# Attention scores in one full-height matmul instead of passes over 32 rows, with heads made four at a time and a loop ordered by a clock model

## The chip, the cores and the metric

The kernel runs on one core of a Trainium2 chip. The metric is the device time of one execution in microseconds, as the median of several runs.

## The reference

Two transformer-like layers work on x of shape (2, 1024, 256), that is 2048 rows of 256 values. Layer 0 is linear attention (16 heads of 16) and a gated feed-forward block with ternary weights, layer 1 is softmax attention with rotary position and a gated feed-forward block whose weights pass a Hadamard transform; each sublayer normalises its input and adds its output to x in the kernel. What this change touches is the attention of layer 1:

```
q = (x @ q_w.T + q_b) in 16 heads of 16; k and v the same; q, k rotated by position
attn  = einsum('bhqd,bhkd->bhqk', q, k) * 16 ** -0.5        # 1024 x 1024 per head
probs = softmax(attn, axis=-1)
out   = einsum('bhqk,bhkd->bhqd', probs, v); then out @ out_w.T + out_b
```

With 2 batches and 16 heads there are 32 such score matrices.

## The kernel before

**Units.** Attention of layer 1 goes by eight units: a batch and a group of four heads (`units`). A unit has 1024 queries, in two halves n of 512, and 1024 keys, in eight blocks of 128. Three kinds of work make one unit.

1. *Search.* For each block of 128 queries, half of the keys and two heads, a score tile `scm` [128 queries, 2, 512 keys] goes to PSUM, and VectorE takes its maximum over the keys (`scores_max`, tile `peak`). There are 32 such pairs of heads in a unit. After 16 pairs `split_peaks` makes the negated maxima into a high and a low fp32r part (`tops`), and `put_peaks` transposes them (tile `mx`).
2. *Weights.* For each block of 128 keys, 512 queries and two heads, the transposed score tile `sce` [128 keys, 2, 512 queries] goes to PSUM with the negated maximum already added, and ScalarE makes `pr` = exp(sce / 4). Again 32 pairs in a unit.
3. *Sums.* `weigh` multiplies `pr` of four heads by the values `va` (16 columns and a one, 17 in all) into four 32-column strips of one PSUM bank, `po`, in fp32. After eight key blocks `po` is transposed back, divided by the sum of weights (`normalise`, `divide`), and after four units of a batch projected by `wo1` (`project`, tile `py<-woT,aT`).

**Exactness.** TensorE handles fp32r in one pass and fp32 in four. q and k are kept as fp32r high and low parts. A head has 32 rows: in `kk` the 16 high and 16 low rows of k; in `qh` the high part of q twice; in `ql` the low part twice. A score tile is then two passes of 32 rows (`qh`, `ql`), and a weight tile three, the third being `ones_r` against `mx`. Four heads lie in the four 32-row strips of the array. `burst` issues the passes of a search pair (two strips) and of a weight pair (the other two) in turns, so that four matmuls run beside each other: ten matmuls in three steps.

**Heads.** `heads_of(b, gg)` makes eight heads (two units) at once, for one block of 128 rows at a time: a projection of 384 columns (`pqkv`), bias on VectorE, rotation on GpSimd and VectorE, splitting, four transposes (`pt`, of `rot` in fp32 and of `ks` in fp32r), then one ScalarE copy to `qk_hi` and one VectorE subtraction to `ql`.

**Order.** Two mechanisms. The front (layer 0 for all but two pieces of its feed-forward, normalisation, the first heads, the whole search of unit 0) is recorded in a `Plan`: `Plan.emit` schedules all recorded operations by their estimated cost, with a table `LEADS` of leads per group and engine. After that comes the loop over units, written out by hand: each step issues a burst for unit u+1's search and unit u's weights, then `slot` fills TensorE with other work in proportion to what is left: `filler` (the rest of layer 0, the Hadamard transforms `pw`, layer 1's feed-forward, tiles `pug` and `py<-wd,hid`), `urgent` (the next heads), `background`, and work due after some steps (`later`). Generators yield marks (SOON, FIRST, SECOND, LAST, PAIR, BOTH) that say at which places of a step they may go on. Two sums are issued after every fourth pair.

**PSUM.** Of eight banks `po` has one, three rotate as `bank`, and two tiles of two banks rotate as `pair`, which scm and sce take in turns.

Every recorded operation is issued in the helper `emit`, so that the profile gives all of them the line L316; the tiles' names tell them apart.

Of the kernel before, what the change touches and what calls it, by code (L numbers as in the profile page):

```python
# [82 lines left out]
BURST = 0.65  # L83
# [15 lines left out]
class Root:  # L99


    def __init__(self, make, n, dtype, ring, before, grain):
        self.make, self.dtype, self.ring, self.before, self.grain = make, dtype, ring, before, grain
        self.tile = None
        self.sums = False
        self.placed = False
        self.ready = np.zeros(n)
        self.writer = np.full(n, -1)
        self.readers, self.adders, self.users = [], [], []
# [48 lines left out]
class Plan:  # L158
    def __init__(self):
        self.ops = []  # L160
        self.open = None
        self.burst = False
        self.group("norm 0a")
        self.holds, self.later = [], set()
# [16 lines left out]
    def add(self, engine, call, name, args, kw):  # L181
        if engine == PE and self.open is not None:
            op = self.open
        else:
            op = Op(len(self.ops), engine, self.leads[ENGINES.index(engine)])
            self.ops.append(op)
            self.open = op if engine == PE else None
            if self.burst:
                op.cost = BURST
# [8 lines left out]
        if not self.burst:  # L198
            op.cost += cost(engine, name, outs[0], ins)
# [72 lines left out]
class Pool:  # L272
# [5 lines left out]
    def tile(self, shape, dtype, tag, name, bufs=None):  # L278
# [9 lines left out]
        )  # L288
        if self.state.plan is None:
            root.get()  # L290
# [3 lines left out]
class Engine:  # L294
# [5 lines left out]
    def __getattr__(self, name):  # L300
        call = getattr(self.engine, name)

        def go(*args, **kw):
            if self.state.plan is None or self.which is None:
                return emit(call, args, kw)
# [5 lines left out]
class State:  # L311
    plan = None

# [5 lines left out]
class Ring:  # L319


    def __init__(self, n, in_order):
        self.places, self.next, self.latest, self.in_order = [None] * n, 0, None, in_order

# [16 lines left out]
def cost(engine, name, out, ins):  # L341
    n = out.ids.size
    if engine == PE:
# [3 lines left out]
        return ins[1].ids.size * (PASS if single else COL)  # L347
# [9 lines left out]

@with_exitstack
def tile_two_layers(ctx: ExitStack, tc: tile.TileContext, a: dict, out: bass.AP):
# [5 lines left out]
    ordered = [False]  # L365
# [10 lines left out]
    ps = open_pool(ctx, "ps", 1, 2 * C, space=PSUM)  # L376
    ident = const.tile([P, P], F32, tag="ident", name="ident")
# [3 lines left out]
    def pair(name):  # L381
        return ps.tile([P, 2, C], F32, tag="pair", name=name, bufs=2)


    taken, in_use, now = [0], {}, [None]

    def has_room():
        return len(in_use) < 3

    def bank(name):  # L390
        while ordered[0] and not has_room():
            go(in_use[min(in_use)])
        t = ps.tile([P, C], F32, tag="bank", name=name, bufs=3)
        if ordered[0]:
            in_use[taken[0]] = now[0]
            t.root.number = taken[0]
            taken[0] += 1
        return t

    def shut(t):  # L400

        if ordered[0]:
            del in_use[t.root.number]

    po = ps.tile([P, C], F32, tag="po", name="po", bufs=1)
    vector.memset(po, 0.0)
# [55 lines left out]
    SOON, FIRST, SECOND, LAST, PAIR, BOTH = 1, 2, 3, 4, 5, 6  # L462

# [26 lines left out]
    def norm_T(src, dst, pause=0.0):  # L490
# [5 lines left out]
        for j in range(CT):  # L496
            vector.bn_stats(stats[:, j, :], src[:, j, :])
            vector.bn_aggr(mv[:, j, :], stats[:, j, :])
            if j == 1:
                yield 0.0, SECOND  # L500
        vector.tensor_scalar_add(rstd, mv[:, :, 1], LN_EPS)
        gpsimd.tensor_tensor(rstd, rstd, minus_half, ALU.pow)
        yield 0.0, SECOND
        vector.scalar_tensor_tensor(shift, mv[:, :, 0], -1.0, rstd, ALU.mult, ALU.mult)
        xn = at.tile([P, CT, D], F32, tag="stage", name="xn", bufs=3)
        for j in range(CT):
# [3 lines left out]
            if j == 1:  # L510
                yield 0.0, SECOND
        yield pause, SECOND
        yield 0.0
        for k in range(2):
            pt = bank("pt")
            for j in range(CT):
                tensor.transpose(pt[:, j * P : (j + 1) * P], xn[:, j, k * P : (k + 1) * P], ident)
            yield CT * P * TR, SOON
            (vector.tensor_copy if k else scalar.copy)(dst[:, k, :], pt)
            shut(pt)  # L520
            yield 0.0


    def ffn(cc, first, second, half_scale, scale, down, before_down):
# [4 lines left out]
        for e in range(NB):  # L529
            cols = slice(e * P, (e + 1) * P)  # L530
            pug = bank("pug").rearrange("p (w n) -> p w n", w=2)
# [13 lines left out]
            yield F * COL, SOON  # L545
# [7 lines left out]
            yield 0.0  # L553
        before_down()
        for j in range(F // P):
            t = at // P + j
            cols = slice(j * P, (j + 1) * P)
            py = bank("py")[:, 0:D]
# [4 lines left out]
            yield D * COL, SOON  # L563
            vector.tensor_add(xc[c][:, t, :], py, xc[c][:, t, :])
            shut(py)
            yield 0.0

    def run(gen):
        for _ in gen:
            pass  # L570

    def cost_of(x):
        return x[0] if isinstance(x, tuple) else x
# [20 lines left out]
    both = at.tile([P, 4, E], F32, tag="qk_hi", name="both", bufs=1)  # L594
    for n, k, m, t, r in (
        ("wuT0", D, E, "wA", both[:, 0:2, :]),
        ("wgT0", D, E, "wB", both[:, 2:4, :]),
        ("wdT0", E, D, "wC", at.tile([P, NB, D], F32, tag="ql", name="wdT0", bufs=1)),
# [11 lines left out]
    trig = load(const, "trig", a["trig"], [P, BT, 2, HD // 2])  # L610
# [139 lines left out]
    def ffn0(cc, before_down, wide=False, by_pool=False):  # L750
# [21 lines left out]
        for e in range(0, NB, step):  # L772
# [4 lines left out]
            else:  # L777
                pug = bank("pug").rearrange("p (w b n) -> p w b n", b=1, w=2)
# [15 lines left out]
            yield 4 * F * PASS, SOON  # L794
# [8 lines left out]
            yield 0.0  # L803
        before_down()

# [12 lines left out]
        yield 2 * D * PASS, SOON  # L818
# [4 lines left out]
        yield 0.0  # L823
# [9 lines left out]
    def norm1(c, pause=0.0):  # L833
        yield from norm_T(xc[c], xnT[c], pause)

        for j in range(0, CT, 2):
            x2 = xc[c][:, j : j + 2, :]
            gpsimd.tensor_tensor(x2, x2, ob1.unsqueeze(1).to_broadcast([P, 2, D]), ALU.add)

# [6 lines left out]
    qh, ql, kk, va, mx = {}, {}, {}, {}, {}  # L846
    late = []

    head_tiles = {}

    def heads_of(b, gg, first=0, last=BT):

        if (b, gg) not in head_tiles:
            pool = late[0] if gg else at
            thk = pool.tile([P, 4, S], F32R, tag="qk_hi", name="qk_hi", bufs=1)
            tl = pool.tile([P, 2, S], F32R, tag="ql", name="ql", bufs=1)
            tv = pool.tile([P, BT, HH, VW], F32, tag="va", name="va", bufs=1)

            gpsimd.memset(tv[:, :, :, HD:], 1.0)
            for i in range(2):  # L860
                g = 2 * gg + i
                qh[b, g], ql[b, g], kk[b, g] = thk[:, i, :], tl[:, i, :], thk[:, 2 + i, :]
                va[b, g] = tv[:, :, 4 * i : 4 * i + 4, :]
            head_tiles[b, gg] = thk, tl, tv
        thk, tl, tv = head_tiles[b, gg]
        half = HD // 2
        w3 = slice(gg * 3 * P, (gg + 1) * 3 * P)
        bias = qkvb[:, w3]

        def lay_out(i, rot, ks):  # L870
            cols = slice(i * P, (i + 1) * P)
            pt = bank("pt").rearrange("p (g n) -> p g n", g=4)
            for g in range(2):
                q4 = rot[:, 4 * g : 4 * g + 4, :, :].rearrange("p h s d -> p (h s d)")
                tensor.transpose(pt[:, g, :], q4, ident)
                k4 = ks[:, 4 * g : 4 * g + 4, :, :].rearrange("p h s d -> p (h s d)")
                tensor.transpose(pt[:, 2 + g, :].bitcast(F32R), k4, ident_r)
            return cols, pt

        def take_out(cols, pt):  # L880
            scalar.copy(thk[:, :, cols], pt)
            vector.tensor_tensor(tl[:, :, cols], pt[:, 0:2, :], thk[:, 0:2, cols], ALU.subtract)
            shut(pt)

        def split_k(i):
            rot, a0, b1 = made[i]
            del made[i][1:]
            vector.tensor_tensor(rot[:, :, :, 0:half], a0, b1, ALU.subtract)
            ks = at.tile([P, HH, 2, HD], F32R, tag="ks", name="ks")
            scalar.copy(ks[:, :, 0, :], rot[:, HH:, 0, :])  # L890
            gpsimd.tensor_tensor(ks[:, :, 1, :], rot[:, HH:, 1, :], ks[:, :, 0, :], ALU.subtract)
            made[i].append(ks)


        made = {}
        for i in range(first, last + 2):
            if i >= first + 2:
                cols, pt = lay_out(i - 2, *made.pop(i - 2))
                yield 3 * P * TR
                take_out(cols, pt)  # L900
            if i >= last:
                yield 0.0, LAST
                if i == last:
                    split_k(i - 1)
                    yield 0.0, PAIR
                continue
            c, j = divmod(b * BT + i, CT)
            qk = at.tile([P, 2 * HH, 2, half], F32, tag="qk", name="qk", bufs=1)
            if state.plan:
                plan.with_place(qk)  # L910
            pqkv = bank("pqkv")[:, 0 : 3 * P]
            for k in range(2):
                tensor.matmul(
                    pqkv,
                    lhsT=xnT[c][:, k, j * P : (j + 1) * P],
                    rhs=wqkv[:, k, w3],
                    start=(k == 0),
                    stop=(k == 1),
                )
                if k == 0:  # L920
                    yield 3 * P * COL
            yield 3 * P * COL, LAST
            if i > first:
                split_k(i - 1)
            yield 0.0, FIRST
            vector.tensor_add(qk.rearrange("p h t f -> p (h t f)"), pqkv[:, 0 : 2 * P], bias[:, 0 : 2 * P])
            vector.tensor_add(
                tv[:, i, :, 0:HD],
                pqkv[:, 2 * P :].rearrange("p (h d) -> p h d", d=HD),
                bias[:, 2 * P :].rearrange("p (h d) -> p h d", d=HD),  # L930
# [3 lines left out]
                trig[:, i, s, :].unsqueeze(1).unsqueeze(1).to_broadcast([P, 2 * HH, 2, half]) for s in range(2)  # L934
# [616 lines left out]
```

## Time and profile before

| what | value |
|---|---|
| median of 3 runs | 870.12 us (868.38 to 872.65) |
| profiled execution | 873.07 us, span 871.3 us |
| mean granted TensorE clock | 0.989 |
| first weight burst (tile sce) | 206.1 us from the span's start |
| last sums of po end | 862.8 us, 8.5 us before the end |

The profile is of one execution. PE is TensorE's matmul row, PEld its weight loads, DVE VectorE, ACT ScalarE, POOL GpSimd, SP SyncE, which issues all DMAs here. A group line ends with busy time and mean duration of one, then the engine's idle time just before these instructions and what ended it. A matmul line of the timeline names the tile that is written and the tiles that are read, and the rows and columns of the array that it uses (32*128 is 32 rows). An fp32 matmul shows as two instructions of two passes. Durations of matmuls overlap, since they are pipelined.

### The profile page before, as it was taken

Reading aid. Unit: us, or ns where it says so; the run is one execution under the profiler, and the core shown is the slowest. Engines: PE = TensorE matmul, PEld = TensorE weight load, DVE = VectorE, ACT = ScalarE, POOL = GpSimd, SP = SyncE. Lnnn points to the kernel's source line nnn. Section 1 sums busy time; section 2 is a strip of 40 time slices with the busy share of each in tenths; the row PEclk is TensorE's granted clock in tenths of the full one; section 3 lists DMA queues with packets and bytes.
Section 4 is the critical chain, followed back from the end, with each engine's and each line's share of the span. In section 5 each row is a group of like instructions: output and inputs, shape, how many; then the busy total and the mean of one; then the engine's idle time right before and its main releaser. Section 6 shows DMA issues by size and latency. Waiting matters only on the chain.

```text
span 871.3 us, 14418 instructions
## 1 busy us (share of the span) xinstructions
PE 840.0 (96%) x5952; PEld 499.5 (57%) x5952; DVE 587.6 (67%) x979; ACT 440.5 (51%) x649; POOL 220.7 (25%) x293
## 2 busy tenths in 40 slices
PE   7999999999999999899999999999999999999997
PEld 5689866576556534555455555555555555555543
DVE  5887665886895687557775767687665666666312
ACT  6745455523664556445553445445454544444663
POOL 2646867621551551103510000045000000000000
PEclk9999999999999999999999999999999999999998
DMA  9200000000000200000000000000100000000001
GB/s 312 91 1 2 2 1 1 1 25 1 1 26 2 97 1 1 1 1 2 1 1 2 1 1 1 1 2 7 43 1 2 1 1 1 2 1 1 1 2 48
DMA packets 10768, 14.88 MB, mean 17 GB/s; under 512 B 1104, under 2 KB 8912, under 8 KB 10704
## 3 DMA queue, kind: packets, MB, share of 16 engines
q1 hardware_dynamic: 10704, 13.98, 4.7%
q8 instruction: 46, 0.75, 0.3%
q14 instruction: 18, 0.15, 0.1%
HBM read 11.88 MB, written 2.10 MB: 16 GB/s over the span
## 4 chain that ended last, share of the span: by engine, by line
PE 81%; DVE 13%; ACT 2%; issue 2%; DMA 1%; POOL 1%; SPq 0%; DVEq 0%; ACTq 0%; POOLq 0%
PE pug L316 17%; PE scm L316 15%; PE py L316 14%; PE po L316 13%; PE sce L316 8%; DVE peak L316 5%; PE pqkv L316 5%; PE pt L316 3%; PE pkv L316 2%; DVE act L316 1%; PE sc L316 1%; PE pq L316 1%; DVE att L316 1%; ACT pr L316 1%; PE pw L316 1%
## 5 line engine op out<-in xcount | busy, mean ns | idle before, releaser
L316 ACT ACTIVATE pr<-sce 128x1024 f32<-128x1024 f32 x256 | 260.6, 1024 | 266.0 <-PE sce L316 265.6
L316 DVE TENSOR_REDUCE peak<-scm 128x2 f32<-128x1024 f32 x224 | 273.9, 1223 | 152.0 <-PE scm L316 149.3
L316 PE MATMUL po<-pr,va 128*17 128x512 f32 x1024 | 124.8, 595 | 0.1
L316 PE MATMUL sce<-qk_hi 32*128 32x512 f32 x512 | 121.7, 497 | 1.1 <-ACT pr L316 0.9
L316 PE MATMUL scm<-qk_hi 32*128 32x512 f32 x448 | 112.5, 498 | 6.5 <-DVE peak L316 5.7
L316 PEld LDWEIGHTS scm<-qk_hi 32*128 32x128 f32 x448 | 41.6, 182 | 116.9 <-DVE peak L316 47.2
L316 POOL CAST tops<-nm 128x16 fp32r<-128x16 f32 x16 | 3.6, 224 | 367.7 <-DVE nm L316 361.7
L316 PE MATMUL sce<-mx,ones_r 32*128 32x512 f32 x512 | 96.6, 393 | 0.1
L316 PE MATMUL sce<-ql,qk_hi 32*128 32x512 f32 x512 | 96.1, 392 | 0.0
L316 PE MATMUL scm<-qk_hi,ql 32*128 32x512 f32 x448 | 89.2, 394 | 0.0
L316 PE MATMUL pug<-xnT,wuT 128*128 128x256 f32 x256 | 73.4, 397 | 0.0
L316 PE MATMUL pug<-xnT,wgT 128*128 128x256 f32 x256 | 70.5, 398 | 3.1 <-DVE xnT L316 1.8
L316 DVE SCALAR_TENSOR_TENSOR act<-act,pug 128x256 f32<-128x256 f32 (+1 forms) x112 | 50.7, 453 | 30.3 <-ACT act L316 24.7
L316 PE MATMUL py<-wd,hid 128*128 128x256 f32 x256 | 66.7, 396 | 0.0
L316 PEld LDWEIGHTS po<-pr,va 128*17 128x17 f32 x1024 | 22.8, 96 | 62.9 <-issue 60.8
L316 PEld LDWEIGHTS py<-wd,hid 128*128 128x128 f32 x256 | 45.1, 189 | 22.8 <-issue 18.4
L316 PEld LDWEIGHTS pug<-xnT,wgT 128*128 128x128 f32 x256 | 45.2, 190 | 22.3 <-issue 15.5
L316 POOL TENSOR_TENSOR hid<-act,hid 128x256 fp32r<-128x256 f32 (+1 forms) x48 | 44.1, 924 | 50.0 <-ACT hid L316 30.9
L316 PEld LDWEIGHTS pug<-xnT,wuT 128*128 128x128 f32 x256 | 46.2, 192 | 17.7 <-issue 12.7
L316 PEld LDWEIGHTS sce<-mx,ones_r 32*128 32x128 f32 x512 | 46.0, 184 | 11.1 <-ACT mx L316 0.5
L316 DVE TENSOR_TENSOR x<-py,x 128x256 f32<-128x256 f32 x68 | 27.5, 418 | 35.7 <-PE py L316 35.5
L316 PEld LDWEIGHTS sce<-qk_hi 32*128 32x128 f32 x512 | 45.4, 182 | 8.3 <-ACT pr L316 5.0
(153 smaller groups left out, 1333.0 us busy)
## 6 DMA issues: line engine op xcount, KB each, us to landing
out<-x SPq DMA_DIRECT2D x16, 128.0 KB, 1.7
x<-in_x SPq DMA_DIRECT2D x3, 512.0 KB, 9.5
both<-in_wuT SPq DMA_DIRECT2D x1, 1024.0 KB, 9.3
both<-in_wgT SPq DMA_DIRECT2D x1, 1024.0 KB, 10.5
wdT<-in_wdT SPq DMA_DIRECT2D x1, 1024.0 KB, 12.9
raw<-in_wdT SPq DMA_DIRECT2D x2, 512.0 KB, 4.3
wgT<-in_wgT SPq DMA_DIRECT2D x1, 1024.0 KB, 4.6
wuT<-in_wuT SPq DMA_DIRECT2D x1, 1024.0 KB, 8.1
```

What stands on the lines that cost most here:

```text
L316: return call(*map(real, args), **{k: real(v) for k, v in kw.items()})
```

## The change

- **One matmul per score tile.** `qk[u]` holds, for each of four heads and for q and k, 64 rows: all four products of the high and low parts (q rows alternate in one way, k rows in another), so that one fp32r matmul gives what two passes gave. Rows 64 to 95 hold ones in k and zeros in q, rows 96 and 97 ones in k and the two parts of the negated maximum in q. Search matmuls read 96 rows, weight matmuls 98. Heads lie beside each other in the free dimension, no longer in strips of the array. `burst`, `ql`, `mx` and the row strips are gone; `po` keeps its four column strips.
- **Heads** are made for one unit (four heads) and two row blocks at a time: projections of 192 columns, one rotation over both blocks, the split before the transposes (tile `hl`), eight fp32r transposes, and two ScalarE copies of 64 partitions for each block into `qk`. The peaks go to rows 96 and 97 by four small ScalarE copies. `borders` sets the constant rows of the two `qk` tiles with eight GpSimd memsets each.
- **Front.** The search in the front is 19 pairs (16 and `LEAD` = 3) instead of 32. The table LEADS is the same.
- **Order of the loop.** `Clock` keeps an estimated time for each engine and for each tile's writes and reads. Generators yield `Ask(views, bank, when)` in place of marks. At each turn the loop compares when a score pair, a sum, or other work could begin by that clock, and takes one. Search pairs run up to 20 pairs ahead of weights, across units. scm and sce have a PSUM tile of their own each. Sums go when two are ready or nothing else is.
- `project` adds and stores two row blocks at a time, and the constant table `trig` is laid out for two blocks.

The instructions of the loop (from the first weight matmul on), counted in the two built programs: TensorE matmuls 3782 before and 2530 after; 1536 + 894 of 32 rows become 512 (sce) + 474 (scm); 512 for po in both.

The core of the diff:

```diff
-BURST = 0.65
+TURN = 0.2
+WEIGH = 0.86
+LEAD = 3
+PRS = 6
+W_GAP = 1.0
...
+class Clock:
...
+        t = self.free[engine]
+        for v in ins:
+            t = max(t, v.root.avail, v.root.wrote[v.ids].max())
+        for v in outs:
+            t = max(t, v.root.avail, v.root.read[v.ids].max(), 0.0 if engine == PE else v.root.wrote[v.ids].max())
+        if engine == PE:
+            if self.kind == "fill":
+                end = t + span(engine, name, outs[0], ins)
+            else:
+                end = t + WEIGH / 4
+            end += TURN / 2 if self.last != self.kind else 0.1 if t > self.free[PE] + 0.06 else 0.0
...
-    def pair(name):
-        return ps.tile([P, 2, C], F32, tag="pair", name=name, bufs=2)
+    def pair(name, tag="pair", bufs=2):
+        return banks[0].tile([P, 2, C], F32, tag=tag, name=name, bufs=bufs)
...
+    def borders(u):
+        for h in range(4):
+            gpsimd.memset(qk[u][2 * HS : 3 * HS + 2, 1, h, :].bitcast(F32), 1.0)
+            yield 0.0
+            gpsimd.memset(qk[u][2 * HS : 3 * HS + 2, 0, h, :].bitcast(F32), 0.0)
+            yield 0.0
...
-            scalar.copy(thk[:, :, cols], pt)
-            vector.tensor_tensor(tl[:, :, cols], pt[:, 0:2, :], thk[:, 0:2, cols], ALU.subtract)
+                cols = slice((i + j) * P, (i + j + 1) * P)
+                for e, put in enumerate((scalar.copy, scalar.copy)):
+                    put(qk[u][0 : 2 * HS, :, e:4:2, cols], pt[2 * HS * e : 2 * HS * (e + 1)])
...
-        for s in range(max(len(passes) for _, passes in scores)):
-            for sc, passes in scores:
-                if s < len(passes):
-                    tensor.matmul(
-                        sc, lhsT=passes[s][0], rhs=passes[s][1], start=(s == 0), stop=(s == len(passes) - 1)
-                    )
+    def scores(i, sc):
...
+        own = slice(0, 3 * HS)
+        for k in range(2):
+            h = 2 * p + k
+            mm(sc[:, k, :], [(qk[u][own, 0, h, qs], qk[u][own, 1, h, ks])])
...
-        scalar.copy(mx[u, n], pt)
+        for h in range(4):
+            scalar.copy(qk[u][3 * HS : 3 * HS + 2, 0, h, n * C : (n + 1) * C], pt[h * HS : h * HS + 2, :])
...
+    def weights(i, sc):
...
+        own = slice(0, 3 * HS + 2)
         for k in range(2):
+            h = 2 * p + k
+            mm(sc[:, k, :], [(qk[u][own, 1, h, ks], qk[u][own, 0, h, qs])])
...
-        for i in range(STEPS // 4):
+        for i in range(8 if part < 2 else LEAD):
...
-                burst(scores_of(u + 1, i + p, scm) + weights_of(u, i, 1 - p, sce))
-                scores_max(u + 1, i + p, scm)
-                prs.append(weights_exp(sce))
...
+        if quota[0] <= 0.2 and s_come <= now + 0.05:
+            choice = "score"
+        elif w_come <= now + 0.1 and both and (s_come > now + W_GAP or room() > 0.0 or quota[0] > 0.2):
+            choice = "sum"
+        elif x_come <= now + 0.1:
+            choice = "fill"
+        elif s_come <= now + 0.1:
+            choice = "score"
```

More of the change, by code (lines that the diff above doesn't have):

```diff
@@ L355, in cost, with span @@
     return n / 472 + (0.19 if n > 16 else 0.8)
+OVER = {PE: 0.0, DVE: 0.083, ACT: 0.105, POOL: 0.05}
+def span(engine, name, out, ins):
+    n = out.ids.size
+    if engine == PE:
+        if name == "transpose":
+            return n * (TR if ins[0].root.dtype == F32 else TR / 2) + 0.003
+        return cost(engine, name, out, ins) + 0.003
+    if engine == DVE:
+        return max([n] + [v.ids.size for v in ins if name == "tensor_reduce"]) / 960 + 0.15
+    if engine == ACT:
+        return n / 1200 + (0.17 if n >= 512 else 0.22)
+    return n / 472 + (0.19 if n > 64 else 0.1)
 @with_exitstack
@@ L593, in tile_two_layers @@
     raw0, tern = {}, {}
-    both = at.tile([P, 4, E], F32, tag="qk_hi", name="both", bufs=1)
+    raw = at.tile([P, 2 * 4, S], F32, tag="qk", name="raw", bufs=1)
+    both = raw[:, 0:4, :]
     for n, k, m, t, r in (
@@ L851, in heads_of @@
[L851 to L865, printed above, removed]
+    late, qk, va, summed = [], {}, {}, [0]
@@ L948, in tile_two_layers @@
+        split = None
+        made = yield from begin(first)
+        for i in range(first + 2, last + 2, 2):
+            following = (yield from begin(i)) if i < last else None
+            if split:
+                yield from turned(*split)
+            split = yield from end(*made)
+            made = following
+        yield from turned(*split)
     hm = load(const, "hadamard", a["hadamard"], [P, P])
@@ L1144, in put_peaks @@
     def put_peaks(u, n):
-        mx[u, n] = late[0].tile([P, C], F32R, tag=f"mx{n}", name="mx", bufs=1)
+        yield Ask(tops, bank=1)
         pt = bank("pt")
@@ new lines, in go, with poll @@
+    def go(gen, queue):
+        x = next(gen, "end")
+        asked[gen] = x if isinstance(x, Ask) else None
+        if isinstance(x, str):
+            queue.remove(gen)
+        elif isinstance(x, float):
+            left[0] -= x
+            quota[0] -= x
+    def poll():
+        for gen in side[:]:
+            if come(gen) <= clock.now() + 0.1 and clock.free[DVE] <= clock.now() + 0.4:
+                go(gen, side)
+        for queue in (quick, urgent, filler):
+            while queue and asked.get(queue[0]) and not asked[queue[0]].bank and come(queue[0]) <= clock.now() + 0.1:
+                go(queue[0], queue)
@@ new lines, in seek, with free_tag, take_come @@
+    def seek():
+        i = sought[0]
+        if i % (2 * PAIRS) == 0:
+            force(urgent)
+        sc = pair("scm", "scm", 1)
+        scores(i, sc)
+        maxima(i, sc)
+        sought[0] += 1
+        if i % PAIRS == PAIRS - 1:
+            u, n = divmod(i // PAIRS, 2)
+            split_peaks(u, n)
+            quick.append(put_peaks(u, n))
+    def free_tag():
+        return "scm" if sought[0] == total and slot("scm") < slot("sce") else "sce"
+    def take_come():
+        i = taken[0]
+        if i == total or sought[0] - i < min(PAIRS + LEAD - 1, total - i):
+            return np.inf
+        u, r = divmod(i, 2 * PAIRS)
+        n = r // PAIRS
+        return max(slot(free_tag()), clock.come([qk[u][:, 0, :, n * C : (n + 1) * C]]), room())
@@ new lines, in take @@
+    def take():
+        i = taken[0]
+        if i % PAIRS == 0 and any(g.__name__ == "put_peaks" for g in quick):
+            force(quick)
+        sc = pair("sce", free_tag(), 1)
+        weights(i, sc)
+        pr = late[0].tile([P, 2, C], F32, tag="pr", name="pr", bufs=PRS)
+        scalar.activation(pr, sc, AF.Exp, scale=HD**-0.5)
+        prs.append(pr)
+        taken[0] += 1
+        if len(prs) == 2:
+            u, r = divmod(i, 2 * PAIRS)
+            pending.append((u, r // PAIRS, r % PAIRS // 2, prs[:]))
+            prs.clear()
+        if i % (2 * PAIRS) == 2 * PAIRS - 1:
+            next_heads(i // (2 * PAIRS) + 2)
+        quota[0] += max(left[0], 0.0) / max(total - 8 - i, 1)
```

662 lines of the change are left out of this document (323 added, 339 removed).

## The prediction

> **What bounds the kernel now.** I read four views: the engines' shares on the page, the groups by form, TensorE's timeline inside the loop, and busy time by stage. Every recorded operation has line L316, a helper, so I go by tiles. First the page:
>
> ```profile
> PE 840.0 (96%) x5952; PEld 499.5 (57%) x5952; DVE 587.6 (67%) x979; ACT 440.5 (51%) x649; POOL 220.7 (25%) x293
> ...
> PE 81%; DVE 13%; ACT 2%; issue 2%; DMA 1%; POOL 1%; SPq 0%; DVEq 0%; ACTq 0%; POOLq 0%
> ...
> L316 ACT ACTIVATE pr<-sce 128x1024 f32<-128x1024 f32 x256 | 260.6, 1024 | 266.0 <-PE sce L316 265.6
> L316 DVE TENSOR_REDUCE peak<-scm 128x2 f32<-128x1024 f32 x224 | 273.9, 1223 | 152.0 <-PE scm L316 149.3
> ```
>
> PE is busy 96% and makes 81% of the chain that ended last. The two large consumers, the maxima on DVE and the exponentials on ACT, wait for PE (149.3 and 265.6 us). So the question is what PE does per score. TensorE's timeline in mid-loop (start, duration, matmul, count):
>
> ```profile
> 487.25 1.91 PE L316 MATMUL po<-pr,va 128*17 128x512 f32 x16
> 489.09 0.50 PE L316 MATMUL scm<-qk_hi 32*128 32x512 f32 x2
> 489.10 0.50 PE L316 MATMUL sce<-qk_hi 32*128 32x512 f32 x2
> 489.43 0.40 PE L316 MATMUL scm<-qk_hi,ql 32*128 32x512 f32 x2
> 489.44 0.39 PE L316 MATMUL sce<-ql,qk_hi 32*128 32x512 f32 x2
> 489.67 0.39 PE L316 MATMUL sce<-mx,ones_r 32*128 32x512 f32 x2
> 489.99 1.13 PE L316 MATMUL pug<-xnT,wgT 128*128 128x256 f32 x4
> 490.96 1.03 PE L316 MATMUL pug<-xnT,wuT 128*128 128x256 f32 x4
> 491.91 0.50 PE L316 MATMUL scm<-qk_hi 32*128 32x512 f32 x2
> ```
>
> Matmul durations overlap, so I read start to start. A burst of ten 32-row matmuls (one search pair, one weight pair) runs four abreast and takes 489.09 to 489.99, 0.90 us. Its middle step, 489.44 to 489.67, is 0.23; the first is 0.34 and the last 0.32. Three steps at 0.215 would be 0.64, so 0.25 is entering and leaving. The eight fp32 instructions of pug that follow take 1.92; at their steady 0.216 they would take 1.73, so a run of fill pays 0.19 too. Two sums (16 po instructions) take 1.84, against 1.71 of streaming: 0.13. Every change between 32-row tiles, full tiles and 32-column tiles thus costs PE about 0.2, and there are 239 score runs, 184 fill runs and 71 po runs in the loop.
>
> Busy time by stage (front, the end of the front, loop, finish):
>
> ```profile
> 0.00:168.00 168.00, 158.74 (x943) 119.96 (x944) 118.45 (x267) 95.41 (x192) 101.42 (x113) 0.99 0.16 53
> 168.00:206.10 38.10, 36.04 (x239) 27.43 (x238) 32.14 (x64) 8.53 (x19) 9.45 (x13) 1.00 0.05 15
> 206.10:861.50 655.40, 640.74 (x4762) 350.10 (x4760) 432.42 (x636) 336.44 (x439) 109.87 (x168) 0.99 0.02 7
> ```
>
> The columns are stretch, PE, weight load, DVE, ACT, POOL. In the loop of 655.4 us DVE is busy 432 and ACT 336; PE is the bound. At 168 to 206 DVE is 84% busy (32 of 38 us), and the chain of waits there runs through the maxima of the first search, two of them here:
>
> ```profile
> 177.76 2.36 DVE peak L316 x2
> ...
> 187.37 2.27 DVE peak L316 x2
> ```
>
> **The loop before, taken apart.** 240 bursts x 0.895 = 215. Sums: 57 visits x 1.84 + 14 single x 0.98 = 119. Fill without its entries, at steady start-to-start times: ffn1 384 matmuls x 0.432 = 166, ffn0 192 x 0.1175 = 23, head projections 48 x 0.646 = 31, head transposes 96 x 0.085 = 8, Hadamard 12 x 0.858 = 10, output projection 28 x 0.432 = 12, small transposes 7; in all 257, plus 184 x 0.2 = 37 of entries. Total 628. The remaining 27 of 655 is PE waiting for something.
>
> **The change, part by part** (counts from the built program's instruction streams).
> - Scores. In the loop 512 matmuls make weights and 474 search; each is one single-pass 512-column matmul over 98 or 96 rows. The trace has none of that height. Lower bound: a 512-column fp32 instruction is two passes and steps by 0.429, so 0.2145 a pass. Upper: the burst's 0.23 step. I take 0.217, near the lower, since that row too is full tiles back to back: 986 x 0.217 = 214 (212 to 227). That equals the 215 of the bursts, though it includes 13 search pairs that the front did before (5.6 us).
> - Entries. The built program gives the new matmuls the same 128x128 tile as the fill; only po keeps 32-column tiles. fp32r next to fp32 in full tiles costs nothing, as the timeline shows in the front, where pkv and pt are fp32 and this pug is fp32r:
>
> ```profile
> 126.84 1.02 PE L316 MATMUL pkv<-wkvT,xnT 128*128 128x512 f32 x2
> 127.30 1.04 PE L316 MATMUL pug<-xs,t_wuT 128*128 128x256 f32 x4
> 128.17 0.64 PE L316 MATMUL pug<-xs,t_wgT 128*128 128x256 f32 x4
> 128.65 1.04 PE L316 MATMUL pt<-ident,xn 128*128 128x128 f32 x8
> ```
>
> From 126.84 to 128.65 is 1.81, and 2 x 0.429 plus 8 x 0.1175 is 1.80: nothing is left for two changes. So only po is set off: 78 visits, each 0.13 plus a re-entry of 0.2, or 26 (lower 78 x 0.13 = 10). Before, entries of fill alone were 37.
> - Sums: 128 x 0.858 = 110, unchanged in work.
> - Fill. Projections of four heads for two row blocks: 112 matmuls of 192 columns x 0.326 = 36.5 (was 31: seven head groups instead of three double ones). Transposes 224 x 0.075 = 17 (was 8); the nearest rows are 0.085 for the fp32r transposes of tops and 0.056, half the fp32 step of 0.109; I take between. Rest unchanged, 218. Total 272.
> - Sum of PE work in the loop: 214 + 26 + 110 + 272 = 622, against 628 with its entries before.
> - Waits. Before 27. The new order chooses by estimated arrival, so I look at what the streams show: between one search pair and the next, PE holds more work than the slot's cycle (0.43 + 0.25 + 1.22 + 0.05 = 1.95) in all but 11 of 236 cases. Against it, 20 transposes of unit 1 stand in a row ahead of its first search, each group behind ACT and POOL copies (some 6 us), and the last 20 weight pairs have little fill (about 5 us behind exponentials of 1.02). I take 20; bounds 5 and 50.
> - Off PE. DVE gets 13 more maxima, 16 us: 432 to about 450. ACT gets 112 copies of 64x512 (nearest row: 128x512 cast of qk_hi, 0.583) and 60 of 2x512 where 24 and 15 such copies stood, so 133 x 0.58 = 77, and splits of about 20: 336 to about 435, 68% of the loop. POOL gets the low halves of both q and k and eight border memsets: 110 to about 165. All lie beside PE; uncovered, ACT's copies are the dear ones (rival B). No DMA is added or moved on SP; project's output goes out in pairs of blocks.
> - Front. PE loses 16 x 0.32 = 5 of projections, the score runs fall from 18 to 38 x 0.217 = 8, and 20 entries x 0.2 = 4 go: 19. DVE loses 13 maxima x 1.22 = 16 where it is 84% busy. The lead table that orders this stretch was left as it is, and POOL gets eight border memsets. 206 becomes 190; bounds 187 (all of it) and 206 (none).
> - Finish: unchanged, 9.8.
>
> Sum: 190 + 622 + 20 + 9.8 = 842 of span, plus 1.8 around it (873.1 less 871.3): 844 on the profiled execution's scale. That execution lay 2.9 above the median of 870.1, so against the median I say 842.
>
> A rule speaks against the change. The Trainium skill, "TensorE: Matmul & The Clock Gate", section "Measured speedup vs the span model", gives 3.07 times for four matmuls of 32 rows run abreast at 512 columns. By that, ten would take about 0.71, an estimate, against 0.87 for four full-height ones, and the loop would lose about 38 us. The row here says 0.90 for the burst among other tiles, and the row decides.
>
> **Rivals.**
> A, slower: the 96 and 98 rows count as a change of tile after all. For it: no matmul of that height is in the trace, and every neighbour that differs in height pays 0.2. Then 629 runs less the 156 changes counted make 473 x 0.2 = 95 more: 937. It decides from 0.06 a change, where the 29 us gain is gone. Against it: the tile in the built program.
> B, slower: ACT becomes the wait. The 133 added copies stand in its fixed queue between exponentials; a score slot that is freed 0.58 late holds PE and all queued behind it. If half hit, 67 x 0.58 = 39, and each stop costs a restart of 0.1: 46, giving 888. It decides from about 40 hits. For it: weight loads already waited 5.0 us for pr; against: ACT idles 266 us before exponentials now.
> C, little: the front keeps its 206 and waits stay at 27: 864.
> D, better: waits of 5 and entries of 10: 810.
>
> **How the numbers follow.** Forecast 0.62 (825 to 862), D 0.10, C with what lies round it 0.13, B 0.11, A 0.04. 814 to 875 leaves out some 0.06 below (part of D) and 0.14 above (most of B, A). Runs here spread over 868.4 to 872.7, so 0.5%, 4.4 us, is about what can be told from no change. Faster by more: 0.62 + 0.10 + 0.09 of C = 0.81; within: 0.04; slower: 0.15 from A and B.
>
> **What would show it.** Right: scm and sce start to start near 0.217, and a fill matmul starting one step after them; po runs still with 0.13; first exponential near 190; PE over 95% busy in the loop; score groups summing to about 214. Wrong: steps of 0.4 beside scores (A); PE's idle time ended by ACT copies of qk (B); a loop start after 200 (C). Wrong altogether if PE's idle time in the loop exceeds 50 us.

## The result and the profile after

The changed kernel takes 911.79 us (median of 4 runs, 910.45 to 918.27) where the kernel before takes 870.74 (4 runs beside it): 1.049 times as long, 95% interval 1.043 to 1.0545. Slower, where I had forecast 842 and faster. The profiled execution took 910.45 us, its span is 908.7, its mean granted clock 0.982. Recorded operations now have the line L375.

From the page: shares of the engines, the chain that ended last, and the groups of the new score matmuls.

```profile
PE 851.9 (94%) x4672; PEld 594.9 (65%) x4672; DVE 574.3 (63%) x939; ACT 534.4 (59%) x825; POOL 256.4 (28%) x345
...
PE 70%; DVE 11%; ACT 9%; POOL 5%; issue 4%; DMA 1%; SPq 0%; ACTq 0%; POOLq 0%; DVEq 0%
...
L375 PE MATMUL scm<-qk 96*128 96x512 f32 x474 | 182.0, 465 | 8.0 <-DVE peak L375 7.5
L375 PE MATMUL sce<-qk 98*128 98x512 f32 x512 | 172.3, 418 | 4.5 <-ACT pr L375 2.3
```

PE still looks like the bound (94%), but its part of the chain fell from 81% to 70%: ACT went from 2% to 9% and POOL from 1% to 5%, so there are stretches in which PE follows others. Which stretches, the busy time by stage tells (front, its end, loop to the last sums; columns as in the prediction):

```profile
0.00:168.00 168.00, 150.42 (x876) 118.75 (x877) 101.02 (x236) 93.14 (x182) 91.46 (x97) 0.98 0.16 53
168.00:214.80 46.80, 38.14 (x217) 30.25 (x215) 27.80 (x60) 16.78 (x38) 17.70 (x27) 0.93 0.04 12
214.80:900.20 685.40, 660.12 (x3574) 444.01 (x3574) 440.92 (x629) 424.51 (x606) 147.26 (x223) 0.99 0.02 7
```

The first weight tile starts at 214.8 (before 206.2, forecast 190). The loop, from there to the end of the last sums, lasts 685.4 (before 656.6). So 8.7 us came in the front and 28.8 in the loop; the finish is unchanged.

In the front PE is busy 188.6 of 214.8 us (150.4 and 38.1), where it was 194.8 of 206.1, and its clock in the second stretch is 0.93 instead of 1.00: it has less to do, waits, and then runs slower as well. By the rows, 150.4 at 0.98 and 38.1 at 0.93 lose about 5.7 us against a full clock, an estimate, where the front before lost 1.6. GpSimd's own waits from 100 us to the loop's start (total, times, longest), and its timeline:

```profile
POOL act L375 <- DVE act L375: 35.4, 12, 11.1
```

```profile
163.88 0.73 POOL L375 TENSOR_TENSOR act<-act,gate 128x256 f32<-128x256 f32 x1 [5.09 <-DVE act L375]
...
165.81 1.41 POOL L375 TENSOR_TENSOR x_sin<-x_qk,trig 128x256 f32<-128x256 f32 x2
```

The rotation of the front's second heads (`x_sin`) stands in GpSimd's queue behind a multiplication of layer 0's feed-forward that waits 5.1 us for VectorE. The last transpose of those heads is at 185.1; nine of the 19 search pairs come after it, and eight of their maxima follow one another at VectorE's pace. The chain of waits runs through them, and earlier through unit 0's eight border memsets, which GpSimd makes in a row:

```profile
61.53 7.02 POOL qk L375 x8
...
188.79 9.14 DVE peak L375 x8
```

In the loop, TensorE's timeline at a steady place:

```profile
681.73 0.76 PE L375 MATMUL scm<-qk 96*128 96x512 f32 x2
682.33 0.60 PE L375 MATMUL py<-wd,hid 128*128 128x256 f32 x2
682.58 0.82 PE L375 MATMUL sce<-qk 98*128 98x512 f32 x2
683.23 0.80 PE L375 MATMUL pt<-ident_r,hl 128*128 128x128 f32 x8
...
684.84 0.63 PE L375 MATMUL sce<-qk 98*128 98x512 f32 x2
685.40 1.91 PE L375 MATMUL po<-pr,va 128*17 128x512 f32 x16
687.24 0.74 PE L375 MATMUL scm<-qk 96*128 96x512 f32 x2
687.81 1.03 PE L375 MATMUL py<-wd,hid 128*128 128x256 f32 x4
```

Fill next to scores costs nothing: `py` and `sce` together take 682.33 to 683.23, 0.90, and two steps of 0.215 plus two of 0.235 are 0.90. (The start of a score after an fp32 fill is recorded early, so read such neighbours together.) Only `po` is set off: the pair before it takes 0.56 instead of 0.47, the visit 1.84 instead of 1.72, the pair after it 0.57. But the step of a score is 0.235, not 0.217.

At one place PE stands still, in unit 1's heads:

```profile
248.06 0.45 PE L375 MATMUL pt<-ident_r,hl 128*128 128x128 f32 x4
251.98 0.49 PE L375 MATMUL pt<-ident_r,hl 128*128 128x128 f32 x2 [3.47 <-POOL hl L375]
...
256.72 0.49 PE L375 MATMUL pt<-ident_r,hl 128*128 128x128 f32 x2 [3.05 <-POOL hl L375]
```

20 transposes that work 1.6 us (eight take 0.64 above) take 10.2 behind GpSimd's subtractions (`hl`). GpSimd's queue is not what holds the second pause: unit 1's last border memset ended at 230.2, and GpSimd itself waits 3.33 us there for ScalarE. ScalarE's and GpSimd's timelines at that place:

```profile
253.20 2.36 ACT L375 CAST qk<-pt 64x512 fp32r<-64x512 f32 x4 [1.77 <-PE pt L375]
255.46 0.71 ACT L375 CAST hl<-rot 128x256 fp32r<-128x256 f32 x2
255.94 1.41 POOL L375 TENSOR_TENSOR hl<-rot,hl 128x256 fp32r<-128x256 f32 x2 [3.33 <-ACT hl L375]
```

It is a ring: PE's transposes release four copies into `qk` on ScalarE, the next halves `hl` (one buffer) stand behind these copies, GpSimd subtracts from them, and PE transposes the result. The two score pairs after the second pause then take 0.98 each (from 258.21 to 260.17) instead of 0.47; the granted clock from 214.8 to 263 is 0.89. Elsewhere the waits are short and many: over the starts of all matmuls, 42 steps in the loop exceed 0.56 us and hold 32.7 us beyond a score's step; before there were 30 with 21.0.

### The profile page after: what moved, and what is told of

The parts are those of the page before. It is cut to its first block, busy times and chain, and to the rows that moved or that the text cites. A ratio compares the mean times of both kernels' runs of the same rounds, so it can differ in the third digit from the quotient of the medians.

```text
span 908.7 us, 12043 instructions
## 1 busy us (share of the span) xinstructions
PE 851.9 (94%) x4672; PEld 594.9 (65%) x4672; DVE 574.3 (63%) x939; ACT 534.4 (59%) x825; POOL 256.4 (28%) x345
## 4 chain that ended last, share of the span: by engine, by line
PE 70%; DVE 11%; ACT 9%; POOL 5%; issue 4%; DMA 1%; SPq 0%; ACTq 0%; POOLq 0%; DVEq 0%
PE pug L375 14%; PE scm L375 12%; PE sce L375 12%; PE po L375 12%; PE py L375 11%; DVE peak L375 4%; ACT qk L375 4%; PE pqkv L375 3%; ACT pr L375 2%; PE pt L375 2%; DVE act L375 2%; PE pkv L375 2%; ACT act L375 1%; PE pq L375 1%; POOL hl L375 1%
## 5 line engine op out<-in xcount | busy, mean ns | idle before, releaser
L375 ACT ACTIVATE pr<-sce 128x1024 f32<-128x1024 f32 x256 | 261.6, 1024 | 230.9 <-PE sce L375 230.1
L375 DVE TENSOR_REDUCE peak<-scm 128x2 f32<-128x1024 f32 x237 | 289.2, 1220 | 136.1 <-PE scm L375 135.5
L375 PE MATMUL scm<-qk 96*128 96x512 f32 x474 | 182.0, 465 | 8.0 <-DVE peak L375 7.5
L375 PE MATMUL sce<-qk 98*128 98x512 f32 x512 | 172.3, 418 | 4.5 <-ACT pr L375 2.3
L375 PE MATMUL po<-pr,va 128*17 128x512 f32 x1024 | 126.0, 598 | 0.0
L375 ACT CAST qk<-pt 64x512 fp32r<-64x512 f32 (+1 forms) x192 | 111.0, 578 | 21.6 <-PE pt L375 18.9
L375 PEld LDWEIGHTS scm<-qk 96*128 96x128 f32 x474 | 81.9, 191 | 61.2 <-DVE peak L375 32.8
L375 PEld LDWEIGHTS sce<-qk 98*128 98x128 f32 x512 | 91.8, 189 | 44.1 <-ACT pr L375 16.6
L375 DVE SCALAR_TENSOR_TENSOR act<-act,pug 128x256 f32<-128x256 f32 (+1 forms) x112 | 51.0, 456 | 95.1 <-ACT act L375 74.3
L375 POOL CAST tops<-nm 128x16 fp32r<-128x16 f32 x16 | 3.5, 216 | 296.4 <-DVE nm L375 296.4
L375 PE MATMUL pug<-xnT,wgT 128*128 128x256 f32 x256 | 72.4, 388 | 2.2 <-ACT qk L375 2.2
L375 POOL TENSOR_TENSOR hl<-rot,hl 128x256 fp32r<-128x256 f32 x64 | 46.0, 739 | 92.7 <-ACT hl L375 92.4
L375 PE MATMUL pug<-xnT,wuT 128*128 128x256 f32 x256 | 71.5, 384 | 0.0
L375 PE MATMUL py<-wd,hid 128*128 128x256 f32 x256 | 66.3, 385 | 0.0
L375 PEld LDWEIGHTS po<-pr,va 128*17 128x17 f32 x1024 | 22.3, 96 | 59.9 <-issue 58.9
L375 POOL TENSOR_TENSOR hid<-act,hid 128x256 fp32r<-128x256 f32 (+1 forms) x48 | 43.8, 918 | 52.9 <-ACT hid L375 52.7
L375 PEld LDWEIGHTS pug<-xnT,wgT 128*128 128x128 f32 x256 | 47.6, 191 | 15.3 <-issue 4.3
L375 PEld LDWEIGHTS py<-wd,hid 128*128 128x128 f32 x256 | 46.9, 189 | 15.6 <-issue 8.5
L375 PEld LDWEIGHTS pug<-xnT,wuT 128*128 128x128 f32 x256 | 47.7, 190 | 8.8 <-issue 0.8
L375 ACT ACTIVATE act<-pug,su_half 128x256 f32<-128x256 f32 (+1 forms) x48 | 26.1, 546 | 43.4 <-PE pug L375 42.7
L375 PE MATMUL pqkv<-wqkvT,xnT 128*128 128x192 f32 x256 | 47.8, 327 | 0.0
L375 PEld LDWEIGHTS pqkv<-wqkvT,xnT 128*128 128x128 f32 x256 | 43.3, 190 | 4.9 <-issue 1.9
```

Source lines behind the costliest of these rows:

```text
L375: return call(*map(real, args), **{k: real(v) for k, v in kw.items()})
```

## Experiments

Each kernel is the changed one with one edit, unless said otherwise, and is compared with the kernel before on the same chip (medians there 869.9 to 872.0).

**The tile alone, in the order of before** (edit of the kernel before):

```diff
-            (sc[:, i, :], [(q[b, g][rows[2 * p + i], qs], kk[b, g][rows[2 * p + i], ks]) for q in (qh, ql)])
+            (sc[:, i, :], [(qh[b, g][:, qs], kk[b, g][:, ks])])
...
-                (sc[:, k, :], [(keys, qh[b, g][r, qs]), (keys, ql[b, g][r, qs]), (ones_r[r, :], mx[u, n][r, :])])
+            made.append((sc[:, k, :], [(kk[b, g][:, ks], qh[b, g][:, qs])]))
```

> The kernel before, in its own order, with one edit: each score tile is one matmul over the 128 rows of its four heads (so scores of heads are mixed, ql and the maxima are left out of the sum). A burst becomes four full-height matmuls instead of ten of 32 rows. Theory 1 (the tile change itself is a gain, its step is twice the 0.1175 of a 256-column fp32r matmul): 240 bursts go from 0.895 to 0.94, +11; some 180 entries of fill at 0.2 go, -36; 71 bursts behind po keep an entry of 0.1, +7; about 852 (845 to 860). Theory 2 (the dearer step or a lasting entry eats the gain): 868 to 885.

Measured: 864.4 (863.2 to 865.6), 0.9937 of before (0.9915 to 0.9959). The loop shrank from 656.6 to 642.2, 14 of the 18 that theory 1 named; the front grew by 6.4, where the planner, with fewer score matmuls to price, ordered the other work otherwise (that this order is the cause, no run shows). The whole lies between the ranges of the two theories, 0.6% under the kernel before and clear of noise. So the step that the change is named after does save a little time; the loss is in what came with it.

**A height that is a tile change**, the search over the first 64 rows:

```diff
-        own = slice(0, 3 * HS)
+        own = slice(0, 2 * HS)
```

> The kernel after with search matmuls over 64 rows instead of 96 (the rows left out are zeros in q, so nothing is lost). The order stays. Theory 1 (96 rows count as the full tile, 64 rows as one of their own): every search pair is set off from what stands beside it at 0.2 on each side, 237 x 0.4 = 95 more, about 1005 (960 to 1020). Theory 2 (the row count sets a matmul off already at 96): no change, 905 to 918.

Measured: 985.75 (two runs, 985.25 and 986.26), 1.132 (1.126 to 1.138): theory 1. TensorE's timeline of this kernel shows what rival A would have looked like:

```profile
507.31 0.73 PE L375 MATMUL scm<-qk 64*128 64x512 f32 x2
507.97 0.73 PE L375 MATMUL sce<-qk 98*128 98x512 f32 x2
508.63 1.91 PE L375 MATMUL po<-pr,va 128*17 128x512 f32 x16
```

Here a pair takes 0.66 where it took 0.47 among full tiles. The loop is 74 us longer, 0.31 for each of 237 pairs; its clock is lower too, 0.969 over the span instead of 0.982, and by an estimate (984.5 x 0.013) some 12 of the 74 are that. 64 rows pay for every change, 96 and 98 rows do not.

**A new lead table** for the front (31 rows, chosen by the planner's own estimate of the front's end; the row of a fourth search part, which this front lacks, is gone; nothing else is edited):

```diff
-    "piece 1": (-242, -206, -275, -311),
+    "piece 1": (-257, -164, -60, -224),
...
-    "heads 1": (-323, -80, -413, -578),
+    "heads 1": (51, 201, -224, -519),
...
-    "search 0": (-842, -831, -846, -843),
+    "search 0": (-1109, -1147, -312, -925),
```

> The kernel after with another table of leads for the front alone, found anew for this change's front by the kernel's own planner; the loop is the same. Theory 1 (the front came 25 us later than forecast because the old table orders GpSimd, VectorE and ScalarE for work that is no longer there): the first weight matmul comes 12 to 20 us sooner than 214.8, at about 197, and the whole gets as much shorter: about 895 (890 to 901). Theory 2 (the split in front of the transposes and the border memsets are simply a longer chain): 906 to 914.

Measured: 898.5 (895.6 to 900.0), 1.031 (1.028 to 1.033), as theory 1 said. The loop starts at 200.5 and is as long as it was (685.3). GpSimd's waits in the same part of the front:

```profile
POOL act L374 <- DVE act L374: 13.7, 9, 3.6
POOL act L374 <- DVE rz L374: 9.0, 1, 9.0
```

The 35.4 became 13.7 and a wait of 9.0 that comes after the last heads; the last transpose of heads is at 156.9 instead of 185.1. The chain of waits now meets one border memset of unit 0 (0.96 us) instead of eight, and the clock in the front's two stretches is 0.99 and 1.00. The table moves the work of every engine at once, so this run shows that the old table cost some 14 us, not which of these waits is worth how much; nor did the kernel before get a newly sought table.

**Unit 1's border memsets on VectorE:**

```diff
-            gpsimd.memset(qk[u][2 * HS : 3 * HS + 2, 1, h, :].bitcast(F32), 1.0)
+            (gpsimd if state.plan else vector).memset(qk[u][2 * HS : 3 * HS + 2, 1, h, :].bitcast(F32), 1.0)
```

(and the same for the zeros)

> The kernel after with unit 1's eight border memsets, at the loop's start, on VectorE instead of GpSimd. Theory 1 (unit 1's heads are late because GpSimd's queue is long there: 7.6 us of memsets ahead of rotation and split; PE waits some 9 us at 20 transposes in a row): 5 to 9 us less, about 905. Theory 2 (the wait comes from the one hl buffer and its copies on ScalarE): 909 to 915.

Measured: 906.6 (903.99 to 910.3), 1.042 (1.0384 to 1.045). The loop is 680.2, 5.2 shorter; the run's interval and that of the changed kernel (1.043 to 1.0545) overlap a little, though each of its four runs is below each of those four. PE's waits for `hl` in the loop fell from 11.0 us in 10 to 3.3 in 6, its waits for the maxima, whose engine now makes the memsets, rose from 7.5 in 16 to 13.8 in 22. TensorE's timeline at one group of unit 1's transposes in this kernel:

```profile
242.69 0.36 PE L375 MATMUL pt<-ident_r,hl 128*128 128x128 f32 x2 [1.42 <-POOL hl L375]
```

So the memsets did delay unit 1's heads: the first of their transposes is at 225.2 instead of 236.5, and fewer are left to stand in a row. Theory 2, the one buffer of `hl` and the copies on ScalarE, is not refuted by this; the second pause in the changed kernel is of that kind. No run has a second buffer; its pool would take 66 kB of a partition where 62.2 are left.

**Both of these:**

> The changed kernel with both edits that helped alone: a new lead table for the front, and unit 1's border memsets on VectorE. Theory 1 (the late front and the transposes of unit 1's heads behind GpSimd are two separate parts of the loss): 200.5 of front plus 680 of loop plus 8 plus 1.8 is 891 (887 to 896). Theory 2 (both give the same waiting back, the search only begins later or earlier): 897 to 903. If the rest of the loss is work and waits of the loop, it stays over 870 in either case.

Measured: 894.8 (893.4 to 895.8), 1.027 (1.024 to 1.030): in theory 1's range. Front 202.2, loop 682.7.

**q and k in bfloat16:**

```diff
-            qk[u] = tile_.rearrange("p (w h) n -> p w h n", w=2)
+            half = (slice(None), slice(None), slice(0, S))
+            tile_ = tile_.then(tile_.ids, "bitcast", mybir.dt.bfloat16).then(tile_.ids, "__getitem__", half)
+            qk[u] = tile_.rearrange("p (w h) n -> p w h n", w=2)
```

(and the border memsets without their `bitcast`)

> The changed kernel with the tiles of q and k in bfloat16 in place of fp32r (scores are then less exact; the number of matmuls, their rows and columns, the copies, the loop's model and its order are kept). Theory 1 (the step of 0.235 belongs to fp32r, and TensorE's stream bounds the loop): the score step falls to about 0.215, the loop by 986 x 0.02 = 20, to 892 (885 to 898). Theory 2 (0.235 is the step of any matmul of this shape, by its weight load or its rows): no change, 908 to 916.

Measured: 890.75 (890.0 to 893.4), 1.024 (1.021 to 1.027): theory 1. The loop is 666.9, 18.5 shorter. TensorE's timeline, and the weight loads of the scores, first of this kernel, then of the changed one:

```profile
501.75 1.91 PE L375 MATMUL po<-pr,va 128*17 128x512 f32 x16
503.60 0.60 PE L375 MATMUL sce<-qk 98*128 98x512 bf16 x2
504.04 1.03 PE L375 MATMUL pug<-xnT,wgT 128*128 128x256 f32 x4
```

```profile
L375 PEld LDWEIGHTS <-qk 98*128 98x128 bf16 (+1 forms) x1024 | 92.8, 98 | 159.9 <-issue 87.9
```

```profile
L375 PEld LDWEIGHTS sce<-qk 98*128 98x128 f32 x512 | 91.8, 189 | 44.1 <-ACT pr L375 16.6
```

A pair takes 0.44, also right after `po`, where the fp32r pair took 0.57. The weight load halves, 98 ns for 189. Two things changed at once, the stream's format and the weight load; which of them makes 0.235 is open. The Trainium skill, "TensorE: Matmul & The Clock Gate", section "Back-to-back issue gap", gives N / 2.4 + 2.5 ns, about 216 ns for 512 columns, as the gap of an isolated matmul; the bfloat16 rows agree (0.44 for two), the fp32r rows do not (0.47). The same section gives about 131 ns for a sustained stream at 512 columns, which no row here reaches. The same page, section "Weight-path perf modes — Fast Weight Load (FWL) and DoubleRow", says that fast weight load is on for 128 weights whose type is not FP32, and was measured at about twice the speed; here that is so for bfloat16 (98 ns) and not for fp32r (189 ns).

**All three:**

> The three edits that helped, together: new lead table, unit 1's border memsets on VectorE, and q and k in bfloat16 (scores are then less exact). Theory 1 (front, unit 1's heads and the fp32r step are separate parts of the loss, and add up): 911.8 less 13, 4 and 21 is 874 (869 to 879). Theory 2 (TensorE that is quicker only waits longer for GpSimd, ScalarE and VectorE, so parts overlap): 880 to 890. In both the changed order and heads stay no faster than the kernel before.

Measured: 871.5 (869.7 to 873.6), 1.0004 (0.9988 to 1.002): theory 1, the parts add up. The first weight tile starts at 201.5 and the loop takes 661.4. The three edits together are worth 40 us, as much as the change lost; the result is level with the kernel before, not faster. The third edit undoes no part of the change: it measures what the fp32r step costs, and since scores in bfloat16 are less exact, it is no replacement.

**Heads of units 1 to 7 left out:**

```diff
-        urgent.append(heads_of(u))
...
+    for u in range(1, len(units)):
+        qk[u], va[u] = qk[0], va[0]
```

(unit 1's border memsets go too, and the loop's account of other work is less by the heads)

> The kernel after with the heads of units 1 to 7 left out (all units use unit 0's q, k and v; the rest is the same). PE loses 54 us of projections and transposes, ScalarE 87 of copies, GpSimd some 105. Theory 1 (most waits of the loop, 49 us beyond work and entries, come from making heads): 912 - 54 - 30 = 828 (818 to 838). Theory 2 (only unit 1's 13 us come from heads, the rest from the cycle of scores): 845 (840 to 853). Theory 3 (heads' work was filler, and without it PE waits for slots): above 855.

Measured: 856.8 (855.5 to 864.4), 0.985 (0.980 to 0.990), just above 855, and 55 less than with heads. That is the heads' work on PE (my 54) and no more, though ScalarE is busy 80 us less in the loop (344.6 instead of 424.5). Waits did not go; they changed owner. PE's waits for the maxima rose from 7.5 us in 16 to this:

```profile
PE scm L375 <- DVE peak L375: 21.7, 29, 3.2
```

**Maxima over half the columns:**

```diff
-        vector.tensor_reduce(peaks[u, n][:, t, kh, 2 * p : 2 * p + 2], sc, AX.X, ALU.max, negate=True)
+        vector.tensor_reduce(peaks[u, n][:, t, kh, 2 * p : 2 * p + 2], sc[:, :, 0:F], AX.X, ALU.max, negate=True)
```

> The kernel after with maxima over half of each score tile's columns (the maximum used is that of half of the keys), 0.69 instead of 1.22 us on DVE; the clock model knows, so the order moves too. Theory 1 (most of the loop's waits in mid-loop are for the search slot that DVE frees, and eight maxima in a row stand at the front's end): waits fall by 20 to 25 and the front by 4 to 8: about 883 (876 to 892). Theory 2 (waits come from ACT and from the heads, DVE only shows as the last releaser): 900 to 912.

Measured: 915.7, 1.052 (1.048 to 1.0555). The front fell to 206.6, as the chain through eight maxima suggests. The loop rose to 700.3, and the whole is above both theories' ranges: the clock model orders by the shorter price, PE's waits for `pr` rose from 2.3 to 6.0 us and for `hl` from 11.0 to 17.6, and the loop's granted clock is 0.98 instead of 0.99. That VectorE's rate sets the loop is not supported, but since the order changed too, this run is no clean test of it.

**The model's price of a score, and the spread of other work:**

```diff
-        return max(0.117, ins[1].ids.size / 2370) if single else ins[1].ids.size * COL
+        return max(0.117, ins[1].ids.size / 2180) if single else ins[1].ids.size * COL
```

> The kernel after with the cost model's single-pass step at 0.235 for 512 columns instead of 0.216 (columns / 2180 instead of / 2370); all work the same, front and loop orders move. Theory 1 (the model's step is only a scale; waits do not come from it): 903 to 915. Theory 2 (pairs are planned too close because of it, and TensorE stops at slots): 885 to 900.

Measured: 911.2, 1.047 (1.043 to 1.050). The model's price of a score (it, too, had 0.216) is not the cause.

```diff
-        quota[0] += max(left[0], 0.0) / max(total - 8 - i, 1)
+        quota[0] += max(left[0], 0.0) / max(total - i, 1)
```

> The kernel after with its other work spread over all score pairs, where it is planned to end eight pairs before the last (total - i instead of total - 8 - i). Theory 1 (the last 30 us lose some 8 to exponentials with nothing beside them): 4 to 8 us less, about 906. Theory 2 (the work has to be done somewhere and another wait takes its place): 909 to 915.

Measured: 914.5 (912.3 to 916.8), 1.049 (1.047 to 1.052): theory 2, no gain.

## Why the prediction was wrong

The terms of the sum against the profile (us):

| term | forecast | measured | difference |
|---|---|---|---|
| front | 190 | 214.8 | +24.8 |
| scores, 986 steps | 214 (0.217) | 231.7 (0.235) | +17.7 |
| entries of po, 78 | 26 (0.33) | 24 (0.09 + 0.12 + 0.10) | -2 |
| sums | 110 | 110 | 0 |
| fill | 272 | 272 (same steps, transposes at 0.080) | 0 |
| waits of the loop | 20 | 48 (685.4 less the four above) | +28 |
| finish | 9.8 | 8.5 | -1 |
| span | 842 | 908.7 | +67 |

- **The front** is the step that failed most. I took off what PE and VectorE no longer do there, and let its upper bound be the old 206, a bound on one side only. But the front is ordered by a table of leads, made for other operations. With the table left as it was, the heads came late and the search after them; a new table took 14.3 us off the front and none off the loop. That GpSimd's queue was what held the heads back is how the profile reads, and is not shown apart from the rest. Against 200.5, another 10 us of my credit is still missing: with the new table PE is busy 12.8 us less than before in the front (182.0 for 194.8), where I took off 19, and it idles 7 us more; why, no run isolates.
- **The score step.** I took the fp32 pass, 0.2145, for fp32r. The row of the right format was quoted in the prediction itself: eight fp32r matmuls of 256 columns at 0.1175, so 0.235 for 512. The bound of 0.23 did not hold it either. Worth 17.7 in the sum; the bfloat16 run gave 18.5 back in the loop, some of it as shorter re-entries after `po`.
- **The waits.** My bounds of 5 to 50 just held the 48, but the value was wrong. About five of them go with GpSimd's memsets ahead of unit 1's heads (5.2 in the loop alone, 2.6 beside the new table). My count of "enough work between search pairs" looked at VectorE's slot alone, and the long waits are on GpSimd, ScalarE and VectorE in turn. Before, the same subtraction leaves 656.6 - 628 = 29, so some 19 are new, and after the memsets' five some 14 have no shown cause: VectorE's maxima (not cleanly), the model's price and the spread of other work were tried, and none of them is it by itself; the ring through ScalarE's copies and the one `hl` buffer was not.
- **What held.** 96 and 98 rows count as full tiles (rival A fell, and the 64-row run shows its price). Only `po` pays for a change. Sums and fill were right, heads with their 54 too. The single matmul gains 14 in the loop in the old order. In the new kernel the loop spends it: heads for four at a time cost PE 15 more (54 for 39), the 13 search pairs moved in cost 6, and the new waits 19. Less 14 that is 26 of the 28.8 by which the loop grew.
- **Rivals.** B named ScalarE's copies. PE's own waits for them in the loop are small (2.2 and 1.8 us, its weight loads' 6.4 and 3.8), but the ring above runs through them, and 4.5% of the chain of waits in the loop, some 31 us, is `qk<-pt` on ScalarE, where the copies before had under 1%. Without heads the 112 large ones of these copies are gone and the waits stay, so B alone is not the loss; no run takes the copies alone away, and their part stays open. C foresaw a front that keeps its time, but not one that loses it; its sign, a loop start after 200, came. The 0.15 that I gave to slower stood on A and B, and the front and the score step, which made most of the loss, were in neither.
- **The test I set** (PE idle over 50 us in the loop) did not trip: PE is busy 660 of 685. Durations of matmuls overlap, so short waits between starts vanish in the busy time; start to start they show. For the same reason "PE over 95% busy in the loop" (it is 96%) was no sign of being right.

## What to carry to other kernels

An order that was tuned for one set of operations is a cost of its own: when a change replaces operations that a table or planner places, forecast a loss in that stretch too, and look for the queue (here GpSimd's) in which the new operations stand behind old ones that wait. Follow a pause through every engine that it names: here GpSimd, named as the releaser, was itself waiting for ScalarE. Take the price of a matmul from a row of the same format, even if its size differs, before one of the same size in another format. Split a change into its edits before judging it: here the tile alone gained, and the heads, the moved work and an old table lost more.

## What the runs showed of the hardware that I had not expected

- An fp32r matmul of 512 columns steps by 0.235 us, a bfloat16 one by about 0.22 (0.44 a pair) and an fp32 pass by 0.2145, all in full tiles; the first fp32r pair after `po` costs 0.10 more, the first bfloat16 pair nothing.
- A pair of 64-row matmuls among full ones costs 0.31 us more on the mean (74 us over 237 pairs, some 12 of them by an estimate a lower clock); at 96 rows, two neighbours of fill and score take the sum of their steps (0.90).
- After two pauses of PE of 3.47 and 3.05 us, score pairs took 0.98 instead of 0.47 for a while; the granted clock of that stretch is 0.89.
